# A graph layer and a two-expert layer: sums of pairs in two PSUM banks, jobs in one piece, dense lots added a pair later

## The chip, the cores and the metric

The kernel runs on one core of one Trainium2 chip, in one launch. The metric is the device time of that core in microseconds (us). A core has a matrix engine (PE, whose weight loads are listed as PEld), a vector engine (DVE), a scalar engine (ACT), GpSimd (POOL) and SyncE (SP), which in this kernel issues most of the plain DMAs. Each engine works off its own list of instructions in order; an instruction that waits holds up all that stand behind it on its engine. Matrix products land in PSUM, which the kernel divides into eight banks of 512 fp32 numbers a partition.

## The reference

Everything is fp32. There are 12500 nodes with 256 features and 200000 edges, sorted by destination, with destinations crowded towards low numbers.

```python
def gnn(X, edge_src, edge_dst, edge_val, W, b):
    support = X @ W
    msgs = support[edge_src] * edge_val[:, None]
    return jax.ops.segment_sum(msgs, edge_dst, num_segments=12500) + b

def ffn(x, Wr, br, W1, b1, W2, b2, gamma, beta):       # x: 1 x 12500 x 256
    w = softmax(mean(x) @ Wr + br)                     # 8 experts, then capacity scaling and softmax again
    top_w, top_i = top_k(w, 2); top_w = softmax(top_w)
    y_e = gelu(x @ W1[e] + b1[e]) @ W2[e] + b2[e]      # 256 -> 512 -> 256
    return layer_norm(sum of top_w * y_e + x, gamma, beta)

x = x + gnn(layernorm(x), src, dst, edge_weight, W, b)
x = x + ffn(layernorm(x), ...)
```

Since the routing uses the mean over all nodes, the same two experts serve every node.

## The kernel before

**Start (to about 100 us).** The normalised rows of x are written to DRAM (`xn`), and the accumulator `acc` (feature by node, all 12500 nodes, in SBUF) is cleared. The kernel sums the normalised rows of an edge's sources first and multiplies by W afterwards.

**Edges.** The 200000 edges make 1563 chunks of 128; four chunks are a super. The first 128 chunks, whose destinations are the lowest and most crowded, are done "dense". The other 359 supers make 180 pairs (the first holds one super), worked off from high destinations to low ones. For each pair, in this order in the loop at L898:
- now and then `prepare_segment` (L314), which works out where a segment of 32 supers lands; a row is spread to all partitions by a product into a scratch bank (L333 to L335), read by ACT (L337) and by DVE (L339, L341);
- `multiply` (L494): a dummy product (L502) and eight products of the gathered rows `g` with a selection matrix (L507), into the bank `pt`, one bank with one buffer; ACT evicts it to `part` (L510);
- `select` for the next pair on DVE (L437) and eight gathers for it on POOL (L486), into the tile `g`, which has three buffers;
- `spread_out` of the pair before (L515): `part` times a placing matrix into `ps` (L522), which DVE adds to `acc` at a place read from a register (L541);
- `dense_steps` (L683), see below;
- `work` (L869) on expert jobs, as far as a budget goes;
- the stages of a finished block of 256 nodes, one stage a pair: `product` (L722: W by L730 into the bank `gz`, L731, statistics and a Newton root on DVE, L86 to L92), `normalised`, `transposed` (L754, again in `gz`, evicted by ACT at L763), `keep` (a DMA to DRAM) and `enqueue`.

**The dense part.** In pairs 1 to 43 three chunks a pair are done. `dense_make` builds two one-hot matrices on DVE (L606, L609), and in the next pair `dense_add` multiplies them (L620) into the bank `dps` (one buffer). Chunks form lots, of four up to chunk 80 and of two after it, which accumulate in the bank; at the end of a lot DVE adds it into a matrix (L634) at a place read from a register. In pairs 45 to 54 that matrix is multiplied by all node tiles (`multiply_tiles`, L656), in pair 54 the result is transposed (`place_dense`), and in pairs 55 to 58 the matrix is cleared.

**Jobs.** After 24 and 38 finished blocks the mean over what is there names an expert, whose weights are loaded. A job is one expert and one block, 98 in all. Its first products make four column groups (`first`, L819: two products a group, L822, into one of two scratch banks `ph`; gelu on ACT, L823). Its second products make two halves (`second`, L825: L830 into the bank `po`; DVE adds the bias and the input, L836, and SP stores the result). `job_steps` (L842) hands these out in pieces with a price: 0.88 us for a column group, and after the second and the fourth, 1.75 us for a half of the job before. A pair's budget is 10.0 − 2.5 − 1.0 = 6.5 us, less 1.9 if a block's product follows and 1.3 if a transpose does; `work` takes pieces while the budget is above zero, and what is overdrawn is carried over.

**Tail.** The last block, the jobs left, the routing, and the mix of the two experts' results with a layer norm, in 25 steps.

PSUM in the loop: one bank each for biases, `gz`, `po`, `pt`, `ps` and `dps`, and two for `ph`.

Of the kernel before, what the change touches and what calls it, by code (L numbers as in the profile page):

```python
# [107 lines left out]
def gnn_ffn_kernel(  # L108
# [155 lines left out]
    with tc.tile_pool(name="rt", bufs=1) as rt, tc.tile_pool(  # L264
# [22 lines left out]
        far = rt.tile([P, 2 * NSEG + 2], FP, name="far")  # L287
        apart = rt.tile([1, NSEG], FP, name="apart")

# [24 lines left out]
        def prepare_segment(k):  # L314
# [17 lines left out]
            nc.vector.tensor_copy(base_i[:, :n], by_group(base)[:, :, 0])  # L332
            bcast = scratch_ps()  # L333
            for i in range(2):
# [30 lines left out]
            nc.vector.scalar_tensor_tensor(gap, gap, float(WIN - NARROW), gap, op0=ALU.subtract, op1=ALU.mult)  # L365
            nc.vector.reduce_max(apart[:, k : k + 1], gap, axis=AX.X)
            t.update(base_i=base_i, rel=rel, slot=slot)

# [64 lines left out]
        selections = {}  # L433
        first_load = -(-DENSE_CHUNKS // DENSE_STEP) + 2
        dense_pairs = first_load + -(-(-(-NQ // 4)) // ROWS_STEP) + 1

# [57 lines left out]
        def multiply(i, g):  # L494

            n = pairs[i][1]
            sel = selections[i][0]
            pt = pps.tile([P, GB, D], FP, name="pt")
            part = partp.tile([P, GB, D], FP, name="part")


            nc.tensor.matmul(  # L502
                pt[:NARROW, 0, : n * SUPER], sel[:, n * SUPER - 1], g[:, : n * SUPER, 0], start=True, stop=True
            )
            for j in range(n * SUPER):
                q = slice(j % SUPER * NARROW, (j % SUPER + 1) * NARROW)
                nc.tensor.matmul(  # L507
                    pt[q, j // SUPER], sel[:, j], g[:, j], start=True, stop=True, tile_position=(0, j % SUPER * NARROW)
                )
            nc.scalar.activation(part[:, :n], pt[:, :n], AF.Copy)  # L510
            return part
# [87 lines left out]

        made, lot_regs = {}, {}  # L600

# [9 lines left out]

        def dense_add(c):

            g = next(g for g, (c0, k) in enumerate(lots) if c0 <= c < c0 + k)
            c0, k = lots[g]
            if c == c0:
                made["ps"] = dps.tile([P, 2 * D], FP, name="dps")
            ps = made["ps"][:, :QW]
            r, q = made.pop(c)
            nc.tensor.matmul(ps, r, q, start=(c == c0), stop=(c == c0 + k - 1))  # L620
            if c == c0 + k - 1:
                if g not in lot_regs:
                    g1 = min(g + NB, len(lots))
# [59 lines left out]
        def dense_steps(i):  # L683

            if i == 0:
                prepare_dense()
                return
            while made_to[1] < made_to[0]:
                dense_add(made_to[1])
                made_to[1] += 1  # L690
# [31 lines left out]
        def product(b):  # L722
# [3 lines left out]
            nc.vector.tensor_tensor(xt, xt, bias_ps[:, 0].unsqueeze(1).to_broadcast([P, TPB, D]), ALU.add)  # L726
            ps = gps.tile([P, TPB, D], FP, name="gz")
            for j in range(TPB):
# [25 lines left out]
        def transposed(b, z):  # L754

            ps = gps.tile([P, H, TB], FP, name="gz")
            for j in range(TPB):
# [60 lines left out]

        def first(k, zT, hT, c):  # L819
            ph = scratch_ps()[:, :TB]  # L820
            for h in range(H):
# [20 lines left out]
        def job_steps():  # L842

            while True:
                fetch()
                if not at_hand:
                    if behind:
                        yield 1.75, behind.pop(0)
                    else:
                        yield None  # L850
                    continue
                k, b, zT = at_hand.pop(0)
                fetch()
                hT = hp.tile([P, FC, TB], FP, name="hT")
                job_open[0] = True
                for c in range(FC):
                    yield 0.88, lambda c=c: first(k, zT, hT, c)
                    if c % 2 and behind:
                        yield 1.75, behind.pop(0)
                made = {}  # L860
                job_open[0] = False
                behind.extend(
                    [lambda h=h, a=(k, b, zT, hT, made): second(*a, h) for h in range(H)]
                )

# [3 lines left out]
        def work(budget):  # L869

            while budget > 0:
                step = next(steps)
                if step is None:
                    break
                step[1]()
                budget -= step[0]
# [21 lines left out]
        for i, (s0, n) in enumerate(pairs):  # L898
# [15 lines left out]
            complete = nxt > 0 and i > 0 and pairs[i - 1][0] <= done_at[nxt]  # L914
            budget = min(budget, 0.0) + PAIR_US - OWN_US - SLACK_US
            budget -= 1.9 * complete + 1.3 * (stage_t is not None)
# [43 lines left out]
        nm = product(0)  # L960
        work(1.5)
        z = normalised(0, nm)
        work(1.5)
        zT = transposed(0, z)
        keep(0, zT)
        work(1.5)

# [41 lines left out]
        def banks():  # L1009

            m, z = lambda: mps.tile([P, TPB, D], FP, name="mix"), lambda: gps.tile([P, TPB, D], FP, name="gz")
            o = lambda: ops.tile([P, TPB, D], FP, name="po")
# [64 lines left out]
        for q in range(len(mixes) + 3):  # L1077
# [10 lines left out]
            if 1 <= q < len(mixes) - 6:  # L1088
                work(2.0)
            elif q == len(mixes) - 6:  # L1090
# [242 lines left out]
```

## Time and profile before

| | |
|---|---|
| median of 3 runs | 2428.95 us (2420.29 to 2430.41) |
| the profiled execution | 2448.85 us |
| its span | 2446.9 us |
| PE busy | 1718.6 us (70% of the span) |
| PE weight loads | 1215.8 us (50%) |
| DVE busy | 1190.5 us (49%) |
| ACT busy | 475.8 us (19%) |
| POOL busy | 1488.0 us (61%) |
| mean granted PE clock | 0.876 of full speed |

An engine's busy time is the time in which it had an instruction under way. In the groups of the profile a line gives the source line, the engine, the operation, what it writes and reads, the shape and the count; then, behind the bars, the busy time and the mean of one in ns, and the idle time of the engine just ahead of these instructions with what ended most of it. In a table of waits a row says which instruction waited for which, for how many us in all, how many times, and the longest. A releaser called "remote" is a signal that no instruction in the trace explains, and "issue" is time in which an engine waited for nothing that the profile shows. The start is over at about 100 us, the last dense lot is added at 671 us, the pairs end at 2265 us, and the last first product of a job (L822) starts at 2315 us.

### The profile page before, as it was taken

What the parts mean: (1) busy time and instruction counts of PE and PEld (TensorE: products, weight loads), DVE (VectorE), ACT (ScalarE), POOL (GpSimd) and SP (SyncE); (2) the same over time, 40 slices, a digit from 0 to 9 for tenths busy, and PEclk for the clock granted to TensorE, in tenths of its full rate; (3) what the DMA queues carried; (4) which work ended last, traced back from release to release, by engine and by line L of the source; (5) the groups of instructions that cost most, each with busy time, mean ns of one, the idle gap of its engine ahead of it and who ended that gap; (6) DMA issues with size and microseconds to landing.
All of it is one profiled execution on the core that took longest, in us unless ns stands there. A gap on an engine that the chain in (4) does not pass through costs nothing.

```text
span 2446.9 us, 29786 instructions
## 1 busy us (share of the span) xinstructions
PE 1718.6 (70%) x9698; PEld 1215.8 (50%) x9698; DVE 1190.5 (49%) x4265; ACT 475.8 (19%) x1085; POOL 1488.0 (61%) x1537
## 2 busy tenths in 40 slices
PE   0056655666567468888888878888887888888775
PEld 0033333333344246656656656566565665565675
DVE  7355555655533544545444444434433433343688
ACT  5201101111101122212122112212121211211233
POOL 5666656665565666666666666666666666665144
PEclk9987767877788779999999989999998999989898
DMA  8533333332375344444444454444444444444486
GB/s 304 193 91 116 103 93 102 109 114 83 116 225 167 110 145 142 136 138 139 141 131 135 138 151 144 133 134 141 133 136 125 137 137 134 130 123 120 160 281 219
DMA packets 167602, 349.17 MB, mean 143 GB/s; under 512 B 33514, under 2 KB 77072, under 8 KB 167440
## 3 DMA queue, kind: packets, MB, share of 16 engines
q0 software_dynamic: 68928, 188.31, 27.2%
q1 hardware_dynamic: 94120, 145.65, 17.6%
q10 hardware_dynamic: 4392, 13.21, 1.4%
q8 instruction: 82, 1.34, 0.2%
q14 instruction: 80, 0.66, 0.1%
HBM read 282.91 MB, written 64.14 MB: 142 GB/s over the span
## 4 chain that ended last, share of the span: by engine, by line
PE 48%; another core or an unknown queue 17%; DVE 16%; issue 12%; ACT 4%; DMA 2%; POOL 1%; SPq 0%; ACTq 0%; DVEq 0%; POOLq 0%
PE ph L822 14%; PE po L830 12%; PE ps L522 5%; PE pt L507 5%; PE dps L620 4%; PE gz L730 3%; DVE st L69 2%; PE dps L662 2%; DVE acc L541 1%; ACT hT L823 1%; ACT xt L393 1%; ACT part L510 1%; DVE nmt L1052 1%; DVE w L609 1%
## 5 line engine op out<-in xcount | busy, mean ns | idle before, releaser
L486 POOL DMA_INDIRECT g<-xn,src_i x1436 | 1368.3, 953 | 810.4 <-issue 394.2
L822 PE MATMUL ph<-zTj,w 128*128 128x256 f32 x1568 | 452.0, 420 | 127.5 <-issue 55.0
L830 PE MATMUL po<-hT,w 128*128 128x256 f32 x1568 | 438.3, 412 | 105.9 <-issue 80.9
L541 DVE TENSOR_TENSOR acc<-acc,ps 128x256 f32 x359 | 151.0, 421 | 678.8 <-remote 293.2
L822 PEld LDWEIGHTS ph<-zTj,w 128*128 128x128 f32 x1568 | 309.9, 208 | 229.0 <-issue 101.7
L830 PEld LDWEIGHTS po<-hT,w 128*128 128x128 f32 x1568 | 314.8, 206 | 197.6 <-issue 125.7
L510 ACT ACTIVATE part<-pt 128x512 f32<-128x512 f32 (+1 forms) x180 | 107.2, 596 | 1145.2 <-remote 596.2
L620 PE MATMUL dps<-w 128*128 128x490 f32 x256 | 151.5, 718 | 146.3 <-DVE acc L634 113.7
L823 ACT ACTIVATE hT<-ph,b 128x256 f32<-128x256 f32 x392 | 178.6, 472 | 311.2 <-PE ph L822 173.2
L448 DVE TENSOR_SCALAR sel<-iota,rel,wgt 128x32 f32<-128x32 f32 x992 | 233.4, 319 | 0.0
L522 PEld LDWEIGHTS ps<-spread,part 128*128 128x128 f32 x1436 | 186.8, 203 | 93.6 <-issue 87.0
L522 PE MATMUL ps<-spread,part 128*128 128x128 f32 x1436 | 223.3, 301 | 11.4 <-DVE acc L541 8.8
L507 PE MATMUL pt<-g,sel 128*32 128x256 f32 x2872 | 219.9, 418 | 0.0
L836 DVE SCALAR_TENSOR_TENSOR yT<-po,b,zTj 128x256 f32<-128x256 f32 x196 | 85.7, 479 | 163.1 <-PE po L830 73.5
L730 PE MATMUL gz<-wg,acc 128*128 128x256 f32 x392 | 120.0, 460 | 49.0 <-remote 15.2
L620 PEld LDWEIGHTS dps<-w 128*128 128x128 f32 x256 | 52.5, 232 | 203.6 <-DVE acc L634 133.8
L502 PE MATMUL pt<-g,sel 128*32 128x8 f32 (+1 forms) x360 | 42.4, 190 | 131.3 <-DMA g<-xn,src_i 71.6
L502 PEld LDWEIGHTS pt<-g,sel 128*32 128x32 f32 x360 | 26.2, 113 | 204.1 <-issue 165.2
L730 PEld LDWEIGHTS gz<-wg,acc 128*128 128x128 f32 x392 | 89.3, 233 | 74.3 <-issue 37.1
L731 DVE TENSOR_TENSOR acc<-gz,xt 128x512 f32<-128x512 f32 x49 | 33.9, 691 | 167.7 <-PE gz L730 107.1
L507 PEld LDWEIGHTS pt<-g,sel 128*32 128x32 f32 x2872 | 98.7, 118 | 26.2 <-issue 8.8
L1044 POOL TENSOR_TENSOR rst<-vet,half 128x4 f32<-128x4 f32 (+1 forms) x25 | 42.4, 1697 | 108.4 <-DVE vet L1042 108.4
(183 smaller groups left out, 1586.6 us busy)
## 6 DMA issues: line engine op xcount, KB each, us to landing
zTj<-zts SPq DMA_DIRECT2D x98, 256.0 KB
yts<-yT SPq DMA_DIRECT2D x98, 256.0 KB
ab<-yts SPq DMA_DIRECT2D x48, 512.0 KB
g<-xn,src_i POOLq DMA_INDIRECT x1436
zts<-zT SPq DMA_DIRECT2D x49, 256.0 KB
xt<-in_x SPq DMA_DIRECT2D x24, 512.0 KB
xn<-xt ACTq DMA_DIRECT2D x24, 512.0 KB
xt<-in_x SPq DMA_DIRECT2D x48, 256.0 KB
```

Of the source, the lines that this page charges most:

```text
L448: nc.vector.tensor_scalar(sel[:, j * SUPER + c], iota[:, :NARROW], t["rel"][:, col], t["wgt"][:, col], ALU.is_equal, ALU.mult,)
L486: nc.gpsimd.indirect_dma_start(out=g[:, j], out_offset=None, in_=xn, in_offset=bass.IndirectOffsetOnAxis(ap=segment[k]["src_i"][:, col : c ...
L507: nc.tensor.matmul(pt[q, j // SUPER], sel[:, j], g[:, j], start=True, stop=True, tile_position=(0, j % SUPER * NARROW))
L510: nc.scalar.activation(part[:, :n], pt[:, :n], AF.Copy)
L522: nc.tensor.matmul(ps[:, j, h], part[:, j, h * P : (h + 1) * P], spread[:, j], start=True, stop=True)
L541: nc.vector.tensor_tensor(at, at, ps[:, j], ALU.add)
L620: nc.tensor.matmul(ps, r, q, start=(c == c0), stop=(c == c0 + k - 1))
L730: nc.tensor.matmul(ps[:, j], node_tile(t0 + j)[:, h], wg[:, h], start=(h == 0), stop=(h == H - 1))
L822: nc.tensor.matmul(ph, w1[:, k, h, c * P : (c + 1) * P], zT[:, h], start=(h == 0), stop=(h == H - 1))
L823: nc.scalar.activation(hT[:, c], ph, AF.Gelu, bias=b1[:, k, c : c + 1])
L830: nc.tensor.matmul(po[:, h], w2[:, k, c, h * P : (h + 1) * P], hT[:, c], start=(c == 0), stop=(c == FC - 1))
L836: nc.vector.scalar_tensor_tensor(yT[:, i], po[:, i], b2[:, k, i : i + 1], zT[:, i], op0=ALU.add, op1=ALU.add)
```

## The change

- The sums of pairs (`pt`) take turns: even pairs use their bank as before, odd ones the bank of the second products (`po`) up to pair 55 and the dense bank after it.
- `dense_add` is divided: `dense_multiply` puts the lots into the two scratch banks in turn, and the additions of the lots that were completed in one pair stand at the head of `dense_steps` of the next pair.
- The row of a segment is spread in the bank `gz`, not in a scratch bank.
- Since a lot's addition can now come after a pair's, each segment also measures whether its pairs near the dense end keep off the dense part's nodes: two more DVE instructions, or one.
- A job is two pieces of 3.5 us: the second products of the job before (both halves), then all four column groups, two to a scratch bank. `work` takes pieces while the budget is above 1.75 us, and carries over up to 1.75 us either way.
- After the dense pairs a block is finished only if no transpose is due in the same pair.
- In the tail three calls of `work` go, and those in the mix ask for 4.0 instead of 2.0.

```diff
-            bcast = scratch_ps()
+            bcast = gps.tile([P, 2 * D], FP, name="gz")
...
+            lo, hi = max(0, low_chunk - s0 * SUPER), min(m, pad)
+            if lo < hi:
+                nc.vector.tensor_scalar(gap[:, lo:hi], base[:, lo:hi], -1.0, float(QH * DENSE), ALU.mult, ALU.add)
+                nc.vector.reduce_max(apart[:, NSEG + k : NSEG + k + 1], gap[:, lo:hi], axis=AX.X)
+            else:
+                nc.vector.memset(apart[:, NSEG + k : NSEG + k + 1], -1.0)
...
-            pt = pps.tile([P, GB, D], FP, name="pt")
+            if i % 2 == 0:
+                pt = pps.tile([P, GB, D], FP, name="pt")
+            elif i > dense_pairs:
+                pt = dps.tile([P, 2 * D], FP, name="dps").rearrange("p (j d) -> p j d", d=D)
+            else:
+                pt = ops.tile([P, H, TB], FP, name="po")
             part = partp.tile([P, GB, D], FP, name="part")
...
-        def dense_add(c):
+        def dense_multiply(c):
 
             g = next(g for g, (c0, k) in enumerate(lots) if c0 <= c < c0 + k)
             c0, k = lots[g]
             if c == c0:
-                made["ps"] = dps.tile([P, 2 * D], FP, name="dps")
+                made["ps"] = scratch_ps()
             ps = made["ps"][:, :QW]
             r, q = made.pop(c)
             nc.tensor.matmul(ps, r, q, start=(c == c0), stop=(c == c0 + k - 1))
             if c == c0 + k - 1:
+                sums.append((g, ps))
+
+        def dense_add():
+
+            while sums:
+                g, ps = sums.pop(0)
...
+            dense_add()
             while made_to[1] < made_to[0]:
-                dense_add(made_to[1])
+                dense_multiply(made_to[1])
...
-        def first(k, zT, hT, c):
-            ph = scratch_ps()[:, :TB]
+        def first(k, zT, hT, made, c):
+            if c % 2 == 0:
+                made["ph"] = scratch_ps()
+            ph = made["ph"][:, c % 2 * TB : c % 2 * TB + TB]
             for h in range(H):
...
             while True:
                 fetch()
-                if not at_hand:
-                    if behind:
-                        yield 1.75, behind.pop(0)
-                    else:
-                        yield None
-                    continue
-                k, b, zT = at_hand.pop(0)
-                fetch()
-                hT = hp.tile([P, FC, TB], FP, name="hT")
-                job_open[0] = True
-                for c in range(FC):
-                    yield 0.88, lambda c=c: first(k, zT, hT, c)
-                    if c % 2 and behind:
-                        yield 1.75, behind.pop(0)
-                made = {}
-                job_open[0] = False
-                behind.extend(
-                    [lambda h=h, a=(k, b, zT, hT, made): second(*a, h) for h in range(H)]
-                )
+                if behind:
+                    yield 3.5, behind.pop(0)
+                elif not at_hand:
+                    yield None
+                if at_hand:
+                    k, b, zT = at_hand.pop(0)
+                    fetch()
+                    hT = hp.tile([P, FC, TB], FP, name="hT")
+                    made = {}
+                    job_open[0] = True
+                    yield 3.5, lambda: [first(k, zT, hT, made, c) for c in range(FC)]
+                    job_open[0] = False
+                    behind.append(lambda a=(k, b, zT, hT, made): [second(*a, h) for h in range(H)])
...
-            while budget > 0:
+            while budget > 1.75:
...
-            budget = min(budget, 0.0) + PAIR_US - OWN_US - SLACK_US
+
+            complete = complete and (i <= dense_pairs or stage_t is None)
+            budget = min(budget, 1.75) + PAIR_US - OWN_US - SLACK_US
...
-                work(2.0)
+                work(4.0)
```

More of the change, by code (lines that the diff above doesn't have):

```diff
@@ L287, in gnn_ffn_kernel @@
         far = rt.tile([P, 2 * NSEG + 2], FP, name="far")
-        apart = rt.tile([1, NSEG], FP, name="apart")
+        apart = rt.tile([1, 2 * NSEG], FP, name="apart")
+        first_load = -(-DENSE_CHUNKS // DENSE_STEP) + 2
+        dense_pairs = first_load + -(-(-(-NQ // 4)) // ROWS_STEP) + 1
+        low_chunk = SUPER * pairs[dense_pairs + 3][0]
         sumc = rt.tile([P, H, NBLK], FP, name="sumc")
@@ L433, in gnn_ffn_kernel @@
         selections = {}
-        first_load = -(-DENSE_CHUNKS // DENSE_STEP) + 2
-        dense_pairs = first_load + -(-(-(-NQ // 4)) // ROWS_STEP) + 1
         def select(i):
@@ L598, in prepare_dense @@
                 nc.vector.reduce_max(far[:, 2 * NSEG + 1 : 2 * NSEG + 2], rel, axis=AX.X)
-        made, lot_regs = {}, {}
+        made, lot_regs, sums = {}, {}, []
         def dense_make(c):
@@ L726, in product @@
             nc.vector.tensor_tensor(xt, xt, bias_ps[:, 0].unsqueeze(1).to_broadcast([P, TPB, D]), ALU.add)
-            ps = gps.tile([P, TPB, D], FP, name="gz")
+            ps = gps.tile([P, 2 * D], FP, name="gz").rearrange("p (t d) -> p t d", d=D)
             for j in range(TPB):
@@ L754, in transposed @@
         def transposed(b, z):
-            ps = gps.tile([P, H, TB], FP, name="gz")
+            ps = gps.tile([P, 2 * D], FP, name="gz").rearrange("p (h t) -> p h t", h=H)
             for j in range(TPB):
@@ L960, in gnn_ffn_kernel @@
         nm = product(0)
-        work(1.5)
         z = normalised(0, nm)
-        work(1.5)
         zT = transposed(0, z)
         keep(0, zT)
-        work(1.5)
         worst = rt.tile([P, 2], FP, name="worst")
@@ L1009, in banks @@
         def banks():
-            m, z = lambda: mps.tile([P, TPB, D], FP, name="mix"), lambda: gps.tile([P, TPB, D], FP, name="gz")
+            m, z = lambda: mps.tile([P, TPB, D], FP, name="mix"), lambda: gps.tile([P, 2 * D], FP, name="gz").rearrange("p (t d) -> p t d", d=D)
             o = lambda: ops.tile([P, TPB, D], FP, name="po")
```

## The prediction

> **What bounds the kernel now.** I read the page's groups first, then the waits, and last the table of stretches, because the share of busy time mixes a dense stage (pairs 0 to 58, up to about 837 us), a job stage (to 2268 us) and a tail. The page's groups:
>
> ```profile
> L486 POOL DMA_INDIRECT g<-xn,src_i x1436 | 1368.3, 953 | 810.4 <-issue 394.2
> L822 PE MATMUL ph<-zTj,w 128*128 128x256 f32 x1568 | 452.0, 420 | 127.5 <-issue 55.0
> L620 PE MATMUL dps<-w 128*128 128x490 f32 x256 | 151.5, 718 | 146.3 <-DVE acc L634 113.7
> L823 ACT ACTIVATE hT<-ph,b 128x256 f32<-128x256 f32 x392 | 178.6, 472 | 311.2 <-PE ph L822 173.2
> ```
>
> The gathers are the backbone: 1436 of them, eight a pair, 0.953 us each with 0.27 us or so of issue between (394.2 over 1436). Eight take about 9.8 us, and a pair takes longer, since the gathers of pair i+3 need the buffer that the product `pt` of pair i has read. The table of stretches with the gathers alone (columns: length, busy time and count on POOL, clock of PE, DMA share, GB/s) gives the time of a pair, length over count times eight:
>
> ```profile
> 150.00:680.00 530.00, 325.96 (x336) 0.77 0.36 106
> 680.00:837.00 157.00, 93.48 (x99) 0.82 0.55 168
> 837.00:2268.00 1431.00, 906.07 (x958) 0.91 0.45 135
> ```
>
> That is 12.62 us a pair in the dense stage (42 pairs), 12.69 while the tiles are multiplied (12.4 pairs), and 11.95 in the job stage (119.75 pairs). In the trace the starts of successive L510 evictions from pair 60 to 178 are 11.87 us apart on the mean, and the tenth and ninetieth percentiles are 11.76 and 11.95: a steady loop, not a chain of accidents. In the dense stage the same percentiles are 7.85 and 17.60. What makes the difference is in the waits of 100 to 840 us (columns: total, times, longest):
>
> ```profile
> POOL g L486 <- PE pt L507: 87.1, 14, 15.5
> PE dps L620 <- DVE acc L634: 113.7, 23, 14.3
> PE pt L502 <- ACT part L510: 21.6, 3, 18.2
> DVE acc L634 <- remote: 17.0, 7, 4.8
> DVE acc L634 <- PE dps L620: 14.3, 8, 3.7
> ```
>
> PE stands before a dense lot until DVE has added the one before it, and DVE stands before that addition until the lot just multiplied is reported. Each closes the loop for the other, and `pt` of the next pair is queued on PE behind both. Between 840 and 2268 us the same table says:
>
> ```profile
> PE ph L822 <- ACT hT L823: 47.6, 42, 3.3
> PE po L830 <- issue: 80.9, 128, 9.7
> PE ph L822 <- issue: 55.0, 94, 1.7
> PE pt L502 <- ACT part L510: 11.6, 1, 11.6
> DVE rel L339 <- ACT base_b L337: 18.2, 3, 7.7
> ```
>
> **The change, part by part.** The profiled execution took 2448.85 us with a span of 2446.9, so 1.95 lie outside; the median of the runs is 2428.95. The sum is made in the profiled execution and its difference taken over to the median (0.8% lower, so differences of some tens of us keep their size).
>
> *Dense lots in the two scratch banks, added a pair later.* The work is the same: 44 additions of 0.666 us, 128 products of two records each. What goes is the round PE, DVE, PE inside a pair. With 3 chunks a pair and lots of 4, three lots in four pairs begin in the pair that ended another, and wait for its addition now; with two banks used by turns I count, by writing out chunks 0 to 11, one wait in four pairs, namely when a lot takes the bank that is added in that very pair. With lots of 2 (chunks 80 to 127, 16 pairs) a pair holds one and a half, so about one wait a pair stays. That addition still stands on DVE behind L541, so the wait that stays is no shorter than L541 makes it. The most to be had is the rate of the job stage: 42 × (12.62 − 11.95) = 28 us. Two thirds of the pairs (26 of 42) have lots of 4, where two waits in three go, and a third have lots of 2, where perhaps half go: 28 × (0.62 × 0.67 + 0.38 × 0.5) = 17 us. Ends: 0 (the product chain of the finished blocks, from L726 through the Newton steps L86 to L92, or L541's wait, is late next) and −28. I take −17.
>
> *`pt` in two banks by turns.* L502 waited 21.6 us in the dense stage and 11.6 later for the eviction of the pair before, in four places. The other 176 pairs show no such wait, and the eviction itself waits for the signal of its own `pt`, so an earlier start of the next `pt` is worth little there. Ends 0 and −33; I take −12, two thirds of the longest (18.2 us, up to 127 us), which stands ahead of everything that follows and can be shortened by no later slack; a third stays out because the eviction ahead of it waits 19 us for its signal all the same. Odd pairs take `po` up to pair 55 (no job runs then) and the dense bank after it (free then, except the placing of pairs 54 to 58).
>
> *Jobs in one piece, four half banks.* Same records: 16 of L822 and 16 of L830 a job, 98 jobs. New is that the four first products lie two to a bank. L337 and L339 both only read one bank, and yet L339 on DVE waits for L337 on ACT (18.2 us, three times, in this stage): accesses of one bank by two engines are put in order here even where no data need it. So I expect the second and the fourth product of a job each to wait for a gelu of 0.472 us and its signals. The trace does not show that wait itself; the nearest row is L822 behind L823, 47.6 over 42, 1.13 us. Ends: 0, if halves are kept apart, and 98 × 2 × 1.13 = 221 us of PE work, of which only what PE has no room for lands on the end. Queued behind it on PE are the rest of the job, the transposes, the product of a block and the next `pt`, for which POOL waits. Does PE have the room? In the job stage successive L822 records start 0.216 us apart, a job is 32 × 0.216 = 6.9 us, and 0.8 jobs go into a pair: 5.5 us. `pt` takes 1.1, the spreading (L522) 1.16, block work about 0.6 on the mean: 8.4 of 11.95 us. The new waits bring 0.8 × 2 × 1.13 = 1.8, so 10.2. On the mean they hide under the gather loop. Pairs in which a block is finished or where first products come ahead of second ones may overrun; I take one pair in five by 0.4 us: +10. Ends −17 (L830 stands 17.1 us behind L836 now, which the new order could end) and +72 (below).
>
> The Trainium skill bears on this: PSUM — Partial Sum Buffer, in "PSUM bank collisions raise a hardware error", asks for guarding by bank and quadrant of partitions, not by address. By that rule the end at 0 falls away and both waits stand in every job; no run here yet shows PE writing one half while ACT reads the other.
>
> *The rest.* The broadcast of a segment moves into the bank `gz`, 12 times; it may wait for L731 or L763, or they for it: 12 × 0 to 1.3 us, hidden by the two pairs or more between the preparation and its first use. Each segment gets two more DVE instructions on one partition, nearest row L366 at 0.274 us: 12 × 0.55 = 7 us of an engine that is 45% busy in the job stage; five fall into the dense stage, +2 there. The SP queue issues the same 98 loads and 98 stores, a store now after both halves as before. In the tail three calls for work go; at the new threshold they would take nothing. Jobs have nearly run out there (last L822 record at 2315 us, and DVE bounds the tail: 140 of 179 us busy). A job left over costs 6.9 us of PE beside it: −3 to +8, I take 0.
>
> The 12.4 pairs of the tile stage (12.69 us each) are touched by no part but follow on the dense loop: ends 0 and 12.4 × (12.69 − 11.95) = −9, I take 0.
>
> Sum: −17 − 12 + 10 + 2 = **−17**: 2432 in the profiled execution and **2412** for the median.
>
> **The rivals.**
>
> *PE becomes the bound (slower).* The room above counts records by their starts. By busy time the page is less kind: in the stretches from 840 to 2268 us PE is busy 1155 of 1428 us, 9.65 us a pair, and stands 136 us more "at issue" (80.9 and 55.0), 1.1 a pair. With 1.8 us of gelu waits that is 12.55 us, over the 11.95 of the gathers by 0.6: 119.75 × 0.6 = +72 us. It decides as soon as PE's own work and waits in a pair exceed 11.95 us; then every `pt` is late and POOL with it. With the gains of −17 − 12 + 2 the time is 2429 + 72 − 27 = **2474**. For it: L339 behind L337, which says that the waits will be there, and that 1.8 of the 2.3 us that PE is not busy in a pair would be eaten. Against it: L510 waits "remote" 596.2 us in 78 cases, so `pt` is now ready long before its eviction can run, and PE may fall back some us without anyone waiting.
>
> *No difference.* The gather loop hides the job waits, and the dense stage keeps its 12.6 us because L541 and the block chain are late next, both still ahead of the additions on DVE: **2427**.
>
> *More than I take.* All of it goes: −28 − 9 − 33 + 2 = −68, with the job waits hidden: **2361**.
>
> Another rule points the other way from the first: Perfetto Trace Analysis, in "Matmuls", wants independent groups to rotate through banks so that evictions overlap. The change does this for `pt` and the lots, and gives it up for the first products. By that rule alone the first two parts gain and the third loses; the trace agrees on the lots (113.7 us) and shows next to nothing to gain on `pt` after the start.
>
> **How the numbers follow.** Forecast (2395 to 2422, about 2412) 0.40; PE the bound 0.34; no difference 0.16; more than I take 0.10. A measurement of this kernel tells about 0.5%, 12 us, from no change. Faster by more: nine tenths of the first and all of the last, 0.46. Within: 0.16 and the remaining 0.04, 0.20. Slower: 0.34. The range must keep most of the second case and half of the last: 2370 to 2480.
>
> **What would show it.** Right, step by step: L620's wait for L634 falls from 113.7 us to under 60; 336 gathers of the dense stage take some 505 to 515 us instead of 530; a new row of L822 waiting for L823 of about 200 × 1 us, while the job stage keeps its 11.9 us a pair. Wrong: L510's "remote" waits shrink to little in the job stage and the pair grows to 12.3 us or more (PE the bound); or L822's waits for L823 don't grow (halves are kept apart); or the dense pair stays at 12.6 us.

## The result, and the profile after

The changed kernel takes 2524.47 us (median of 4, 2516.05 to 2534.7) against 2424.62 us of the kernel before (4 runs, 2408.52 to 2430.41): 1.0425 times as long, 95% interval 1.0358 to 1.0491. The forecast was 2412, the range 2370 to 2480. The profiled execution took 2534.7 us with a span of 2532.8, 85.9 more than the span before. Every ratio here is taken over runs within 1.5% of their kernel's fastest, which leaves out two of the four runs of a6_late, in experiment 9.

The groups of the page after, with L494 the gathers (L486 before), L845 and L853 the first and second products (L822, L830), L846 the gelus (L823), L634 the dense lots (L620) and L654 their addition (L634 before):

```profile
L494 POOL DMA_INDIRECT g<-xn,src_i x1436 | 1368.4, 953 | 891.5 <-issue 391.2
L845 PE MATMUL ph<-zTj,w 128*128 128x256 f32 x1568 | 459.3, 431 | 325.1 <-ACT hT L846 183.7
L853 PE MATMUL po<-hT,w 128*128 128x256 f32 x1568 | 380.6, 394 | 8.5 <-issue 7.9
L634 PE MATMUL ph<-w 128*128 128x490 f32 x256 | 149.6, 719 | 99.1 <-DVE acc L654 82.7
```

The gathers cost the same and stand idle 81 us longer. PE's idle time ahead of first products has grown from 127.5 to 325.1 us and now ends with a gelu; ahead of second products it has all but gone (8.5 us, 105.9 before). The gathers by stretch (length, busy time and count, clock, DMA share, GB/s), cut where the stages end:

```profile
150.00:680.00 530.00, 333.73 (x345) 0.78 0.37 110
680.00:827.00 147.00, 86.42 (x91) 0.83 0.55 168
827.00:2347.00 1520.00, 905.87 (x958) 0.89 0.42 127
```

The last row holds as many gathers as its partner before, 958, in 1520 us instead of 1431: 12.69 us a pair instead of 11.95. By the starts of the evictions of pair sums (L524), pair 3 is 8 us earlier than before, pair 15 level, pair 45 14 us earlier (666 against 680), pair 58 10 earlier (827 against 837) and pair 179 82 later (2347 against 2265); the tail takes 4 more. So **−10 in the dense stage, +92 in the job stage, +4 behind it: +86**.

The waits of 840 to 2347 us, PE's and then POOL's (total, times, longest; L521 are the products of a pair's sum, L507 before):

```profile
PE ph L845 <- ACT hT L846: 181.0, 108, 17.1
PE ph L845 <- issue: 128.8, 83, 17.2
...
PE po L853 <- issue: 7.9, 21, 0.9
```

```profile
POOL g L494 <- PE pt L521: 118.8, 18, 22.7
POOL g L494 <- remote: 109.1, 57, 3.4
POOL g L494 <- PE dps L521: 81.8, 19, 12.6
```

POOL's before, from 840 to 2268 us:

```profile
POOL g L486 <- remote: 143.6, 66, 3.5
POOL g L486 <- PE ph L822: 80.9, 38, 2.3
...
POOL g L486 <- PE pt L507: 13.2, 3, 5.0
```

Issue aside, POOL's waits in this stage add up to 260 us before and 354 after: 95 us, about what the stage lost. PE waits up to 17.1 us for an answer that takes 0.47 us to work out (the row put down to issue holds gaps of the same kind, up to 17.2), and POOL waits up to 22.7 us for a pair sum, 5.0 before: the loss is no even thinning of PE's time. Measured from the first gather of one pair to that of the next (pairs 60 to 179), the median is 11.76 us, a little *less* than before (11.85). But 15 pairs take over 13.5 us where 2 did, and the time beyond 11.95 us in a pair adds up to 121 us where it was 9.

One such pair, in the chain of work between 936 and 976 us (start, length, what; "another core or an unknown queue" is a wait for a signal that no instruction of the trace explains):

```profile
934.80 7.01 another core or an unknown queue
...
942.49 9.88 another core or an unknown queue
952.37 0.02 issue
952.39 0.48 ACT hT L846
952.87 0.04 issue
952.92 3.80 PE ph L845 x8
956.72 0.02 issue
956.74 0.48 ACT hT L846
957.22 0.04 issue
957.26 2.08 PE ph L845 x4
959.34 4.29 PE po L853 x16
```

The first of the four products was recorded at 934.8 to 935.8 us, but ACT learned of it only at 952.4. The second product, in the same bank, had to stand for that gelu; behind it stood the rest of the job, a block's product, a segment's row and the next `pt`, which started at 972. Over all 98 jobs the gap behind the first product adds up to 235 us and behind the third to 78 (by the starts of records and the modelled ends). Seventeen gaps over 3 us hold 166 of the 235, and **all seventeen are jobs whose first product stands directly behind `pt` and `ps`**: there are 64 such jobs, with a mean gap of 3.16 us. In the 32 jobs with second products between, the mean is 0.99 and the longest 2.58; the last two lie in the tail. What such a gap costs goes by its length: eight are over 10 us, each stands just ahead of a pair of its own among the 15 slow ones, and these eight pairs hold 90 of the 121 us. Of the nine gaps of 3 to 7 us only two (4.0 and 4.3 us) stand at a slow pair, both under 13.8 us. Five slow pairs, of 13.7 to 15.8 us, have no gap over 3 us behind a first product.

### The profile page after: what moved, and what is told of

Its sections match the earlier page's. It is cut to its first block, busy times and chain, and to the rows that moved or that the text cites. A ratio compares the mean times of both kernels' runs of the same rounds, so it can differ in the third digit from the quotient of the medians.

```text
span 2532.8 us, 29696 instructions
## 1 busy us (share of the span) xinstructions
PE 1693.6 (67%) x9698; PEld 1211.9 (48%) x9698; DVE 1191.7 (47%) x4281; ACT 490.1 (19%) x1085; POOL 1488.6 (59%) x1537
## 3 DMA queue, kind: packets, MB, share of 16 engines
q1 hardware_dynamic: 94120, 145.65, 17.1%
## 4 chain that ended last, share of the span: by engine, by line
PE 50%; another core or an unknown queue 16%; DVE 15%; issue 11%; ACT 5%; DMA 2%; POOL 1%; SPq 0%; ACTq 0%; DVEq 0%; POOLq 0%
PE ph L845 16%; PE po L853 12%; PE ps L536 5%; PE ph L634 4%; PE gz L751 3%; ACT hT L846 2%; PE pt L521 2%; DVE st L69 2%; PE dps L521 2%; PE dps L682 2%; DVE acc L555 1%; ACT xt L403 1%; ACT part L524 1%; PE gz L780 1%
## 5 line engine op out<-in xcount | busy, mean ns | idle before, releaser
L494 POOL DMA_INDIRECT g<-xn,src_i x1436 | 1368.4, 953 | 891.5 <-issue 391.2
L845 PE MATMUL ph<-zTj,w 128*128 128x256 f32 x1568 | 459.3, 431 | 325.1 <-ACT hT L846 183.7
L845 PEld LDWEIGHTS ph<-zTj,w 128*128 128x128 f32 x1568 | 307.1, 210 | 448.7 <-ACT hT L846 239.6
L853 PE MATMUL po<-hT,w 128*128 128x256 f32 x1568 | 380.6, 394 | 8.5 <-issue 7.9
L853 PEld LDWEIGHTS po<-hT,w 128*128 128x128 f32 x1568 | 307.5, 200 | 62.4 <-issue 18.2
L846 ACT ACTIVATE hT<-ph,b 128x256 f32<-128x256 f32 x392 | 185.6, 473 | 551.0 <-PE ph L845 299.6
L634 PE MATMUL ph<-w 128*128 128x490 f32 x256 | 149.6, 719 | 99.1 <-DVE acc L654 82.7
L524 ACT ACTIVATE part<-pt 128x512 f32<-128x512 f32 (+1 forms) x90 | 53.5, 594 | 442.7 <-remote 240.0
L634 PEld LDWEIGHTS ph<-w 128*128 128x128 f32 x256 | 54.3, 232 | 156.8 <-issue 111.1
L521 PE MATMUL pt<-g,sel 128*32 128x256 f32 x1432 | 110.4, 420 | 0.0
L524 ACT ACTIVATE part<-dps 128x512 f32<-128x512 f32 x62 | 37.0, 597 | 318.7 <-remote 195.0
L516 PE MATMUL pt<-g,sel 128*32 128x8 f32 (+1 forms) x180 | 21.2, 190 | 108.0 <-issue 80.8
L516 PEld LDWEIGHTS pt<-g,sel 128*32 128x32 f32 x180 | 13.0, 113 | 141.4 <-issue 111.5
```

The lines of the kernel that those rows point to most:

```text
L494: nc.gpsimd.indirect_dma_start(out=g[:, j], out_offset=None, in_=xn, in_offset=bass.IndirectOffsetOnAxis(ap=segment[k]["src_i"][:, col : c ...
L521: nc.tensor.matmul(pt[q, j // SUPER], sel[:, j], g[:, j], start=True, stop=True, tile_position=(0, j % SUPER * NARROW))
L845: nc.tensor.matmul(ph, w1[:, k, h, c * P : (c + 1) * P], zT[:, h], start=(h == 0), stop=(h == H - 1))
L846: nc.scalar.activation(hT[:, c], ph, AF.Gelu, bias=b1[:, k, c : c + 1])
L853: nc.tensor.matmul(po[:, h], w2[:, k, c, h * P : (h + 1) * P], hT[:, c], start=(c == 0), stop=(c == FC - 1))
```

## The experiments

**How the chips differ.** The runs fell on several chips, and these are of two kinds. On four of them the kernel before takes 2088 to 2091 us, and a pair with the old jobs takes 10.0 in the traces taken there (b3_pt), the bare pace of the gathers (8 × 1.25 us). On two it takes 2442 to 2450, near the 2424.62 on that of the result, where a pair of it takes 11.9. Every run is compared with the kernel before on its own chip. "Quick" and "late" stand below for the two kinds of chip.

**1. The jobs alone.** The kernel before, with `job_steps`, `first`, the budget, the rule on finished blocks and the tail of the change:

```diff
-            ph = scratch_ps()[:, :TB]
+            if c % 2 == 0:
+                made["ph"] = scratch_ps()
+            ph = made["ph"][:, c % 2 * TB : c % 2 * TB + TB]
...
-                for c in range(FC):
-                    yield 0.88, lambda c=c: first(k, zT, hT, c)
-                    if c % 2 and behind:
-                        yield 1.75, behind.pop(0)
+                    yield 3.5, lambda: [first(k, zT, hT, made, c) for c in range(FC)]
```

> The kernel before with only the jobs of the change (second products in one piece, then four first products in half banks, the new budget, the tail's calls). Theory A (the jobs carry the loss, because a first product that stands right behind the pair's products cannot report its end while gathers run, and the next product of its bank waits for that): 90 to 115 us over before, with some 15 to 20 waits of more than 3 us behind the first of the four. Theory B (the sums of pairs in the dense and second-product banks carry the loss): within 15 us of before.

Measured on a quick chip: 2091.75 against 2087.93 us, 1.0023 (1.0012 to 1.0034). Neither theory could show itself there.

**2. The changed kernel itself on a quick chip.**

> The changed kernel itself, beside the kernel before on the same chip. In the four runs of the job before this one a pair took 10.0 us instead of 11.9, and the end of a pair's product was reported at once. Theory A (the loss comes from late reports of first products behind the pair's own products): where a pair takes 10 us the loss is small, 0 to 25 us; where it takes 11.9 us it is 90 to 110 us again. Theory B (the order of the jobs fills PE up by itself): the loss is as large or larger where a pair takes only 10 us, over 100 us, since PE has less room there.

2102.29 against 2088.22 us, 1.0071 (1.0053 to 1.0089): 14 us, as theory A has it. PE's first line of waits from 697 to 1914 us, and the gathers in that stretch:

```profile
PE ph L845 <- ACT hT L846: 112.0, 192, 0.9
```

```profile
697.00:1914.00 1217.00, 915.16 (x966) 0.97 0.53 160
```

192 waits are two a job for 96 jobs, 0.58 us each, and none is over 0.9: most gelus start 0.04 to 0.1 us after the product that they wait for, the latest 0.37. The pair takes 10.08 us. The same two waits a job that come with a loss of 92 us on the late chip are nearly hidden here.

**3. The other parts alone, on a quick chip**: the lots in the scratch banks, added a pair later (b2_dense), and the turns of the pair sums (b3_pt). From the edit of b2_dense:

```diff
-                made["ps"] = dps.tile([P, 2 * D], FP, name="dps")
+                made["ps"] = scratch_ps()
...
+            dense_add()
             while made_to[1] < made_to[0]:
-                dense_add(made_to[1])
+                dense_multiply(made_to[1])
```

> The kernel before with only the dense lots in the scratch banks, added a pair later (with the segment's row in the other bank and the two more instructions a segment). Where a pair takes 11.9 us: 5 to 20 us under before, by the prediction's term of 17. Where a pair takes 10 us: theory C (the gathers leave no room that an earlier addition could win, and the additions that now stand first on DVE delay what is behind them): 0 to 10 us over before; theory D (the round between PE and DVE still costs there): 5 to 15 us under.

> The kernel before with only the turns of the pair sums. The prediction's term is 12 us under before, nearly all at the start. Rival: the dense bank, which odd sums take after pair 55, and the bank of the second products, which they take before it, bring no wait and no gain: within 4 us.

The lots: 2094.93 against 2088.22, 1.0035 (1.0022 to 1.0048), 7 us slower: theory C. The pair sums: 2089.12, 1.0004 (0.9994 to 1.0014): nothing, the rival. Why the lots win nothing is in the waits of 100 to 560 us of both; for b3_pt, whose dense part is that of before, L625 multiplies a lot and L639 adds it:

```profile
POOL g L486 <- issue: 107.1, 352, 0.3
...
PE dps L625 <- DVE acc L639: 60.0, 29, 5.2
```

and for b2_dense, with L629 and L649:

```profile
PE ph L629 <- DVE acc L649: 52.1, 20, 6.2
```

The times of the wait fall from 29 to 20, its sum only from 60 to 52 us, and POOL was not waiting for it in the first place: its idle time is issue. What grew in b2_dense are PE's waits ahead of a pair's sum for what DVE makes: 46 us (21.0 for `sel`, 14.6 for `w`, 10.7 for `spread`) against 28 (16.9, 5.4, 5.6) in b3_pt, which agrees with theory C's delay on DVE.

**4. The changed kernel with the old jobs** (both of the last parts together), on two quick chips.

> The changed kernel with the jobs, budget and tail of before; lots, their later addition and the turns of the pair sums stay. Theory A: 5 to 25 us under before, 2400 to 2420. Theory B: over 2500.

> The changed kernel with the jobs, budget and tail of before. Where the pair takes 11.9 us: the prediction's terms of 17 (lots) and 12 (pair sums) less 2 say 10 to 35 us under before; the rival, that the loop of late reports stays what it was and takes these back, says within 10 us of before. Where it takes 10.0 us, 9 us over, as measured there.

1.0046 (1.0032 to 1.0061) and 1.0047 (1.0030 to 1.0064): 8 to 9 us slower than before, the lots' 7 and what one can't tell from nothing. Neither fell on a late chip, so what these parts are worth there was not measured by themselves.

**5. Every first product in a bank of its own**, in the changed kernel (a1) and with the jobs alone (b5, c2):

```diff
-            if c % 2 == 0:
-                made["ph"] = scratch_ps()
-            ph = made["ph"][:, c % 2 * TB : c % 2 * TB + TB]
+            ph = scratch_ps()[:, :TB]
```

> The changed kernel with each of the four first products in a bank of its own (two banks in turn) instead of two to a bank. Theory A1 (late reports of the first product): the third product now waits for the gelu of the first, so the waits over 3 us stay, about 17 of them and 150 us, and only the short ones go: 2490 to 2520. Theory A2 (two waits a job of about a microsecond each fill PE up): nearly all of the loss goes, 2410 to 2435.

> The kernel before with the jobs of the change, but every first product in a bank of its own. Where reports are late: theory A1 keeps most of the loss, 50 to 110 us over before, since the third product waits for the gelu of the first; theory A2 says within 15 us. Where reports come at once: within 6 us of before, since the gelu of the first runs beside the second product.

> The same, with every first product in a bank of its own. Where the pair takes 11.9 us: theory A1 (what hurts is the late report of the first product, and the third now waits for its gelu) 50 to 110 us over before; theory A2 (the waits that the half banks add are the whole loss) within 20 us. Where it takes 10.0 us, 1 us, as measured there.

On quick chips: a1 1.0047 (1.0031 to 1.0063), b5 1.0006 (0.9996 to 1.0016), c2 1.0002 (0.9992 to 1.0012), while the jobs with half banks, run again beside c2, gave 1.0020 (1.0010 to 1.0030):

> The kernel before with only the jobs of the change, again, for a chip on which a pair of the kernel before takes 11.9 us (the four chips' runs until the last two had 10.0). Theory A: 70 to 115 us over before, with 10 to 20 waits of over 3 us behind the first product of a job. Theory B: within 15 us. Where the pair takes 10.0 us, 4 us over, as measured there.

So on a quick chip the half banks cost 3 us (c1 against c2) to 5 us (the changed kernel against a1), and the order of the products nothing that shows. The expectations for late chips remain open with these runs.

**6. Never a first product directly behind the pair's sums**: second and first products in one piece of 7.0 us, in the changed kernel.

```diff
-                    yield 3.5, behind.pop(0)
...
-                    yield 3.5, lambda: [first(k, zT, hT, made, c) for c in range(FC)]
+                    yield (7.0 if old else 3.5), both
```

> The changed kernel with the second products of the job before and the first ones of this job always in one piece of 7.0 us, so that no first product stands right behind the pair's own products; the half banks stay. Theory A1: the waits over 3 us behind the first product go (none, or a few), the short ones of about 0.8 us stay, the job stage comes back to 11.9 to 12.1 us a pair: 2415 to 2445. Theory A2: the two waits a job are still there, and the time stays over 2490.

> The changed kernel with second and first products of a job always in one piece of 7.0 us, so that no first product stands right behind the pair's own products. Where the pair takes 11.9 us: theory A1, the waits over 3 us behind the first product are gone but for a few, and the time is at least 40 us under the changed kernel's (which is 4.2% over before there); theory A2, no better than the changed kernel. Where it takes 10.0 us, 2.6% over before, as measured there.

On quick chips 1.0256 (1.0234 to 1.0279) and 1.0242 (1.0225 to 1.0259), worse than the changed kernel's 1.0071: here the piece itself does harm. A pair takes 10.3 us, and POOL, which in the changed kernel there waited 6 us for pair sums (5 times), now waits 36 us for them (25 times in c3, from 860 us on, up to 6.9 us). This points to a whole job in one pair being more than PE has room for. That says nothing on late reports.

**7. PE's own pace**: from pair 111 on, odd pairs gather nothing.

```diff
+            if i > 110 and i % 2:
+                return last_g[0]
```

> The changed kernel, but from pair 111 on odd pairs gather nothing and use the rows that the pair before has gathered (so their sums are made of other rows: part of the work is left out). Theory A (a product's end is reported late only while gathers run): where a pair took 12.6 us, late reports go in the quiet pairs, and pairs 111 to 179 fall to 10 to 11 us, bound by PE; the first products of a job show no wait over 3 us there. Theory E (late reports have nothing to do with the gathers): they stay, and the pair stays over 12 us. Where a pair takes 10 us already (no late reports), PE then sets the pace: 8.5 to 10 us, with PE busy over 95%.

On a quick chip. Since the sums differ, so does the naming of experts, and the kernel then runs its general path behind the usual one, which makes the time as a whole (88386 us) meaningless; the pairs can be read. From pair 120 to 160 one takes 9.85 us, and PE (first column) is busy 90% of the time:

```profile
1300.00:1500.00 200.00, 179.20 (x1124) 136.05 (x1123) 97.56 (x385) 50.33 (x111) 75.62 (x80) 1.00 0.36 110
```

PE's waits for gelus take 20 us more, which makes up the 200. So PE alone sets 9.9 us a pair with the changed jobs at a granted clock of 1.00, close under the gathers' 10.0 and 2 us under the late chip's 11.9 (where the clock was 0.89 in the job stage). On the mean there was room. Theory A and E could not be told apart, since nothing was late there.

**8. More room for the gathers**: seven buffers of four chunks instead of three of eight, in the kernel before.

```diff
-        gp = open_pool(name="gat", bufs=3)
+        gp = open_pool(name="gat", bufs=7)
```

> The kernel before with the gathered rows in seven buffers of four chunks instead of three of eight, so that the gathers can run half a pair further ahead. Where a pair takes 11.9 us because its third buffer waits for a late report: theory F (the report comes when the gathers pause for want of a buffer, wherever that is) says the pause only moves, 11.5 to 11.9 us a pair and within 60 us; theory G (the report has a delay of its own of some 5 us) says half a pair more cover brings the pair to 10.0 to 10.8 us and the time down by 130 to 250 us. Where a pair takes 10.0 us already, nothing: within 10 us.

On a quick chip 0.9998 (0.9989 to 1.0008): nothing, as expected there. F and G stay open.

**9. Answers made late by hand.** ACT reads each pair sum seven times more, from pair 60 on, ahead of the eviction that counts. All that stands behind on ACT comes 4.2 us later. The four kernels fell on late chips, two by two.

```diff
+            for _ in range(7 if i > dense_pairs + 4 else 0):
+                again = latep.tile([P, GB, D], FP, name="again")
+                nc.scalar.activation(again[:, :n], pt[:, :n], AF.Copy)
             nc.scalar.activation(part[:, :n], pt[:, :n], AF.Copy)
```

> The kernel before, but from pair 60 on ACT reads each pair sum seven times more into a spare tile ahead of the eviction that counts (7 x 0.6 = 4.2 us), so that everything that stands behind it on ACT, the gelu of a first product above all, answers PE about 4 us later: a late answer made by hand, for chips where none occurs. Theory A (the order of before has other products between a first product and the next user of its bank): at most 40 us over the plain kernel before.

> The changed kernel with the same seven readings ahead of each eviction from pair 60 on. Theory A (in the changed order the second product of a job waits at once for the gelu of the first, with nothing between): about two in three of the 98 jobs have their first product right behind the pair's own products and stand up to 4 us longer, 64 x 3 to 4 us = 190 to 260 us of PE, of which at least 60 us reach the end beyond what the same readings cost the kernel before. Theory A2 (only the number of waits matters, not what a late answer does to them): the same cost as in the kernel before, within 20 us.

> The kernel before with only the jobs of the change (half banks), and with the seven more readings of each pair sum by ACT from pair 60 on, which make answers from ACT 4.2 us later. Where a pair takes 11.9 us: 220 to 300 us over the kernel before, like the changed kernel with these readings (which was 293 over), so the jobs alone carry it. Where a pair takes 10.0 us: PE's own 9.7 us a pair plus about two thirds of 0.8 jobs times 3.5 us make 11.5, so 120 to 230 us over before.

> The same with every first product in a bank of its own. Theory A1 (the order is the weakness: the third product still stands for the gelu of the first, with one product of 0.9 us between instead of none): at least half of the cost of the kernel with half banks stays. Theory A2 (the half banks are the weakness): the cost falls to that of the kernel before with these readings, 33 us where a pair takes 11.9 us, under 50 us anywhere.

| with late answers | us | the plain kernel before, same chip | ratio (95%) |
|---|---|---|---|
| before (b6) | 2475.41 | 2441.95 | 1.0111 (1.0062 to 1.0160) |
| changed (a6, two runs) | 2708.95 | 2441.95 | 1.1087 (1.1006 to 1.1168) |
| before, with the new jobs (d1) | 2749.83 | 2449.74 | 1.1219 (1.1162 to 1.1276) |
| the same, full banks (d2) | 2612.49 | 2449.74 | 1.0672 (1.0601 to 1.0742) |

The same 4 us cost the old order 33 us and the changed kernel 267 (the 293 of an expectation above is by the median of all four, 2734.98). With the jobs alone it is 300, so **the jobs by themselves make the kernel sensitive**, and the lots and the turns of the pair sums need not be there for it. Full banks take the 300 to 163: about half is the sharing of a bank, and about half stays with the order, second products out of the way and the third product dependent on the gelu of the first. Beyond the 33 that the readings cost in the old order, full banks keep 130 of the 267 that the half banks cost (300 less 33), 49%, so "at least half" of A1 can't be told from just under it; A2 falls. PE's wait for gelus from 858 to 2310 us in b6, d1 and d2 in this order (PE's line; total, times, longest). The pairs of d1 run on to 2563 us and those of d2 to 2424, so these two rows leave out the end of their stage:

```profile
PE ph L826 <- ACT hT L827: 107.6, 32, 4.8
```

```profile
PE ph L828 <- ACT hT L829: 248.7, 80, 9.2
```

```profile
PE ph L826 <- ACT hT L827: 196.0, 49, 12.3
```

Pairs of over 13.5 us from first gather to first gather: 3 in b6, 67 in d1, 50 in d2.

## Why the prediction was wrong

*Jobs in one piece: forecast +10, measured +92.* This is the step that failed. Its count was right: two waits a job, as the ordering of L339 behind L337 let expect, and 192 of them where they can be counted cleanly, on a quick chip (0.58 us each there, not 1.13). So the Trainium skill's rule in PSUM — Partial Sum Buffer, "PSUM bank collisions raise a hardware error", to guard by bank, was the right reading of this program; the number beside it is those 192 waits, and the time of 1.0002 with full banks (c2). The room was right on the mean, too: 10.2 us of PE work and waits a pair were reckoned, 9.9 measured on a quick chip (a4). Wrong was the price of a wait: I took the mean of a row (1.13 us) of an order in which other products stood between, and spread it evenly. On the chip of the result a report behind `pt` comes late, and the prediction knew it: L510's 596.2 us of "remote" waits are named in it as a reason that PE can fall back unnoticed. I didn't see that the same late reports would now stand inside PE's own chain. The old order puts another product and a half of the job before between almost every first product and the next user of its bank, so lateness cost little (47.6 us in 42 waits); the new one asks twice a job with nothing between, directly behind the late ones in two jobs of three. Seventeen gaps hold 166 us, the eight longest of them stand at eight pairs with 90 us too much, and the term that was put at +10 measured +92.

*PE becomes the bound (2474).* Right in its sign and its place, wrong in its mechanism, so that it lies nearer than the forecast is in part luck. PE's busy share fell, from 81% of 840 to 2268 us to 75% of 860 to 2340 (1114 of 1480 us). The median pair didn't get slower. Its sign came half true: the pair grew to 12.69 us, but the eviction's `remote` waits, which were to shrink to little, are still 361.4 us (448.7 before, both in the job stage). PE isn't full; it stands.

*Dense lots: −17.* PE's wait for the addition fell from 113.7 to 82.7 us (forecast: under 60), and the dense pair from 12.62 to 12.29 us (530 over 345, times eight; the forecast of 505 to 515 us for 336 gathers was 516). At pair 58 that is worth 10 us in the two profiled executions. But ahead of the readings a6 comes 9 us later than b6 at pair 58 (a6's trace is of a run of 2751.83 us). Over all late traces pair 58 comes at 837, 840, 841 and 858 us with the old lots and at 827 and 867 with the new, and on quick chips this part costs 7 us. A gain is not established; it is small either way.

*`pt` by turns: −12.* Pair 3 comes 8 us earlier, in both pairs of traces from late chips (which change the lots as well), and by pair 15 the kernel is level or behind again; why was not measured. Alone the turns are worth nothing on a quick chip (1.0004). What I charged for the 18.2 us wait did not reach the end.

*The rest: +2, tail 0.* The tail took 4 us more; the single items were not measured.

The rule that I set against the first, the Trainium skill's Perfetto Trace Analysis, "Matmuls" (independent groups should rotate through banks), is borne out where the first products are concerned: 3 to 5 us on quick chips, and 137 of 300 us with late answers. For `pt` it brought nothing on a quick chip.

What stays open: the new jobs were not run by themselves on a late chip without the added readings, so that they carry the +92 there rests on the stage, on the seventeen gaps and on the runs with late answers together. Full banks and the single piece of 7.0 us were not run on a late chip without the readings either. Why reports are late on some chips, and whether they would come at once without gathers, was not settled. In each of the six late traces the eight gelus behind the last gather start within 0.04 us of their product, which fits reports that come at once without gathers, but they are few.

## What to carry to other kernels

A wait's price is not the mean of the row that shows it today: ask what stands between the product and the next user of its bank, and what the wait would cost if the answer came as late as the latest answers in the trace. Where a profile shows long "remote" waits that nobody pays for, keep round trips between engines out of the busy engine's list, or put other work between the question and the answer. Idle time on the mean is no room if the waits fall into few pairs: here gaps of up to 7 us were mostly hidden, and gaps of over 10 us were not.

## What the runs showed of the hardware

The same program took 2088 to 2091 us on four chips and 2424 to 2450 on three occasions on others, with the same mean duration of a gather (0.95 us) and the same median of a record of a first product (0.38 us) in the traces. What differs is how soon a product's end is reported. In the same kernel, the changed one, the eviction of pairs 60 to 178 starts 0.15 us (median and longest) after the pair's last product, or after ACT is free if that is later, on a quick chip, and 2.5 us (up to 14.7) on that of the result; in the kernel before it was 5.1 us there. In the case shown the report of a first product behind a pair's sum came 17 us late. It fell into a break of 0.8 us between the packets of two gathers, but such breaks of 0.6 to 0.9 us stand between most gathers of that stretch, so this explains nothing. The mean granted clock differs too, 0.91 to 0.92 for the kernel before on quick chips and 0.86 to 0.89 on late ones; what follows from what was not tested.

After a long stand PE's granted clock is lower. The changed kernel from 936 to 960 us (PE, PEld, DVE, ACT and POOL busy; then the granted clock):

```profile
936.00:942.00 6.00, 0.00 (x0) 0.00 (x0) 0.73 (x4) 0.11 (x1) 4.30 (x5) 0.87 0.56 156
942.00:953.00 11.00, 0.08 (x1) 0.08 (x1) 0.84 (x2) 0.96 (x2) 7.55 (x8) 0.50 0.37 107
953.00:960.00 7.00, 6.44 (x15) 4.65 (x16) 0.00 (x0) 1.42 (x3) 0.00 (x0) 0.50 0.00 0
```

The clock falls to 0.50 while PE stands, and is still 0.50 in the 7 us in which it works off the job. Behind all seventeen gaps of over 3 us the mean clock of the next 7 us is 0.50 to 0.76 (0.50 in eleven); behind gaps under 1 us it is 0.98 on the mean. So a part of the 92 us can be slower work behind the gaps; how much was not measured.
